# Storing the outputs of layer 1's chunks 0 to 6 tile by tile instead of a chunk at a time

## The chip, the cores and the metric

The kernel runs on one core of one Trainium2 chip. The metric is the device time of one execution in microseconds (us); the median of several runs is compared. The profile shows one more execution, taken by the hardware profiler, with the core's engines: PE (TensorE matmul), PEld (TensorE weight load), DVE (VectorE), ACT (ScalarE), POOL (GpSimd) and SP (SyncE, which here only issues DMAs and waits).

## The reference

Two transformer-like layers with adaptive layer norms run on `x` of shape 4 x 1024 x 256 (batch, sequence, features), all in f32. Each layer adds a gated attention-like part and a gated mixture of experts to `x`. Cut to what matters:

```python
# layer 0: an attention without softmax, then a mixture of 8 experts (256 -> 1024 -> 256), top 2
x = x + ga * _L0_attn_ref(h, L0_attn_queries, L0_attn_combiners)
...
x = x + gb * _L0_ffn_ref(h, L0_ffn_W1, L0_ffn_b1, L0_ffn_W2, L0_ffn_b2, L0_ffn_Wr, L0_ffn_br)
...
# layer 1: fast weights over 8 chunks of 128 positions; a chunk's loss shrinks the weights for the next
h = _layernorm(x, axis=-1) * (1 + ca) + sa
x = x + ga * _L1_attn_ref(h, L1_attn_w0, L1_attn_w1, L1_attn_w2)
# then a mixture of 8 experts (256 -> 256), top 2, each output plus its probability, times its weight
h = _layernorm(x, axis=-1) * (1 + cb) + sb
x = x + gb * _L1_ffn_ref(h, L1_ffn_router_w, L1_ffn_expert_weights)
return x
```

The last line is what concerns us: the sum `x + gb * ...` of layer 1's experts is the kernel's output, 4 MB.

## The kernel before

**Tiling.** The sequence is cut into 8 chunks of 128 positions, one position per partition. `x` stays in SBUF in the tile `x_sb`, `[P, NC, B, D]` with P = 128 partitions, NC = 8 chunks, B = 4 batch entries and D = 256 features. A chunk is thus four tiles of 128 x 256 f32, 128 KB each, and 512 KB together. In the output's layout, `out[b, c*P : (c+1)*P, :]`, a tile is one contiguous piece of 128 rows of 1 KB.

**Stages.** Layer 0's attention comes first; then its experts run over blocks of 128 gathered rows, up to about 626 us into the span. Layer 1 goes through the chunks in order: `combine` finishes layer 0's output for the chunk, `normal` makes the layer norm, `fast` the fast weights, and `routed` picks each position's two experts. The rows of chunks 0 to 3 form a first group of (position, expert) pairs, `ga`, those of chunks 4 to 6 a second, `gb`. When a group is complete (after chunks 3 and 6), `closed` sorts its pairs by expert and `block` handles them 128 rows at a time: POOL gathers the rows, PE multiplies them by the expert's weights, ACT copies the result, and SP stores it to memory (L2289). After all blocks of a group, `combine` with the key `"c2"` brings the results home, tile by tile: two gathers by POOL (L332), a scaling by ACT (L1504), and on DVE a weighted sum (L1510), the gate (L1513) and the addition to `x_sb` (L1515). `combine` returns a list `done` with one entry per tile, the planner's piece for these DVE steps. Chunk 7 is done without gathers by `dense`: all 8 experts on all its rows, weighted on DVE (L2340, L2349), gated (L2369) and added to `x_sb` (L2370), and each of its four tiles is stored behind its own addition (L2373).

**The order of work.** Layer 1's instructions are handed to a planner, the class `Plan`. A piece has an engine, an assumed duration, the pieces it comes after, the buffer slots it holds, a rank and a lag. `Plan.run` steps through a simulated time: at each step every free engine starts the ready piece of lowest rank whose slots are free. The pieces are then issued in the order of their planned starts, and each engine, SP's queue included, executes in that order. SP takes 0.1 us for a store in this plan. Waits between engines follow from the data: SP's DMA waits for a semaphore that the writing engine raises.

**The output stores.** In the last loop, the stores of chunks 0 to 3 get ranks from 6.4 on and those of chunks 4 to 6 from 8.2 on. Each of these seven stores comes after the whole list `done` and carries the chunk's four tiles in one DMA:

```python
plan(SP, 0.1, store, after=done, rank=(6.4, 8.2)[which] + 0.2 * (q - first))
```

The store of chunk 6 is SP's last DMA. Behind it stand the closing waits, drains and barriers of the program (L2525 in the profile).

Of the kernel before, what the change touches and what calls it, by code (L numbers as in the profile page):

```python
# [19 lines left out]
P = 128  # L20
B, S, D = 4, 1024, 256
# [117 lines left out]
def adaln_d2_kernel(  # L139
# [20 lines left out]
    nc = tc.nc  # L160
# [22 lines left out]
    x_sb = const.tile([P, NC, B, D], F32, name="x_sb")  # L183
# [58 lines left out]
    rank = const.tile([P, E], F32, name="rank")  # L242
# [7 lines left out]
    for dst, sign, op in ((upto16, 1, ALU.is_ge), (past16, -1, ALU.is_gt)):  # L250
        nc.gpsimd.affine_select(
            out=dst,
# [8 lines left out]
    def iota(name, pattern, shape, base=0, mult=0, mask=None, pool=const):  # L261
# [21 lines left out]
        out=below16,  # L283
# [595 lines left out]
    plan = Plan(p1=3, p2=2, pm=3, xn1=5, h1T=2, xn2=6, h2T=2, t1=1)  # L879
# [422 lines left out]
    q = plan("SP", 0.1, gates_out, after=rows_done, rank=-0.8, lag=2.2)  # L1302
# [14 lines left out]
    for half in range(2):  # L1317
# [8 lines left out]
        rank_ = max(SECONDS) - 0.3  # L1326
# [33 lines left out]
    d = of_batch["turned"]  # L1360
# [3 lines left out]
    def bases():  # L1364
# [3 lines left out]
    d = plan(DVE, 3.9, lambda: g0.close_staged(pa), after=[m], holds=[ps], rank=-1.0)  # L1368
# [4 lines left out]
        after=[m2],  # L1373
        holds=[ps2],
        rank=-0.9,
# [4 lines left out]
    d = plan(DVE, 1.4, lambda: g0.limits(pa), after=[m, bs], holds=[ps], rank=-1.0)  # L1380
    plan(DVE, 1.2, lambda: g0.list_weights(pa), after=[d], holds=[ps], rank=-0.75)
    for j in range(AHEAD):
# [11 lines left out]
        first = -1.0 + 0.1 * j  # L1394
# [47 lines left out]
    SP = "SP"  # L1442
# [320 lines left out]
    plan = Plan(rings=RINGS, **room1)  # L1763
# [184 lines left out]
    plan = Plan(rings=RINGS, **room1)  # L1948
# [199 lines left out]
    def shares(g, c, at, vb, x, rank):  # L2148

        key = ("m", c)  # L2150

        def do():
            x = made[key, "x"]
            down = tiny([P, B, E + 1], "rdown")
            nc.vector.tensor_scalar(down, x, -1.0, 1.0, ALU.mult, ALU.add)
            nc.vector.reciprocal(down, down)
            nc.vector.scalar_tensor_tensor(x, x, 1.0, down, ALU.add, ALU.mult)
            p = tiny([P, 2, B], "rp")
            nc.vector.tensor_reduce(p[:, 0, :], x[:, :, :E], AX.X, ALU.add)
            nc.vector.reciprocal(p[:, 0, :], p[:, 0, :])  # L2160
            nc.vector.tensor_tensor(
                p[:, 1, :].unsqueeze(2), x[:, :, E : E + 1], p[:, 0, :].unsqueeze(2), ALU.mult
            )
            total = tiny([P, B], "rtotal")
            nc.vector.scalar_tensor_tensor(
                total, p[:, 0, :], 1e-6, p[:, 1, :], ALU.add, ALU.add
            )
            nc.vector.reciprocal(total, total)
            w = g.w[:, :, at : at + B]
            nc.vector.tensor_tensor(  # L2170
                w, p, total.unsqueeze(1).to_broadcast([P, 2, B]), ALU.mult
            )
            nc.vector.tensor_tensor(p, p, w, ALU.mult)
            nc.vector.tensor_tensor(vb[:, at : at + B], p[:, 0, :], p[:, 1, :], ALU.add)

        return plan(DVE, 2.2, do, after=[x[0]], holds=[x[1]], rank=rank)
# [5 lines left out]
    def closed(g, after, rank):  # L2182

        key = g.name
        ps = plan.slot("pm")

        def turn():
            made[key, "turn"] = g.turn(ps_m, 0)

        def bases():  # L2190
            made[key, "bases"] = g.bases(ps_m)

        def ranks():
            made[key, "ranks"] = g.ranks(ps_m)

        m = plan(PE, 0.3, turn, after=after, holds=[ps], rank=rank)
        t = plan(
            ACT, 0.7, lambda: g.turned(made[key, "turn"], 0), after=[m], holds=[ps], rank=rank
        )
        ps = plan.slot("pm")  # L2200
        m = plan(PE, 0.15, lambda: g.total(ps_m), after=[t], holds=[ps], rank=rank)
        d = plan(DVE, 2.3, lambda: g.close(late), after=[m], holds=[ps], rank=rank)
        ps = plan.slot("pm")
        m = plan(PE, 0.15, bases, after=[t], holds=[ps], rank=rank)
        b = plan(
            ACT, 0.2, lambda: g.based(made[key, "bases"]), after=[m], holds=[ps], rank=rank
        )
        ps = plan.slot("pm")
        m = plan(PE, 0.4, lambda: g.across(ps_m), after=[d], holds=[ps], rank=rank)
        e = plan(DVE, 0.2, g.list_experts, after=[m], holds=[ps], rank=rank)  # L2210
        d = plan(DVE, 1.1, lambda: g.limits(late), after=[e, b], holds=[ps], rank=rank)
        ps = plan.slot("pm")
        m = plan(PE, 0.3, ranks, after=[t], holds=[ps], rank=rank + 0.3)
        s = plan(
            DVE,
            0.8,
            lambda: g.places(late, made[key, "ranks"]),
            after=[m],
            holds=[ps],
            rank=rank + 0.3,  # L2220
        )
        s = plan(DVE, 0.8, lambda: g.slots(late), after=[d, s], rank=rank + 0.5)
        return d, e, s

    def block(g, j, rows, y, lists, experts, stored, rank):
# [65 lines left out]
        m = plan(PE, 0.87, mm, after=[a], holds=[xTs, p2], rank=rank)  # L2291
        a = plan(ACT, 0.45, out_, after=[m], holds=[p2, ys], rank=rank - 0.2)
        s = plan(SP, 0.35, store, after=[a], holds=[ys], rank=rank - 0.2)
        return moved(0.5, [s], rank - 0.4, [ys], 1.6)

# [91 lines left out]
    for c in range(NC):  # L2387
        if c in firsts:
            slot, slotT, ts = plan.slot("h1"), plan.slot("hT1"), []
            plan("BEFORE", 0.0, lambda: None, holds=[slot, slotT], rank=-9.0)  # L2390
        else:
            sums = combine(
                "c1",
                c,
                "yg1",
                None,
                g0,
                lambda b, c=c: c * B + b,
                None,
                gb0,  # L2400
                [],
                c - 1.3,
                2.7,
            )
            slot, slotT, hs, ts = normal(
                ("n1", c), c, "1", [[d] for d in sums], (SHA, SCA), c - 1.2, [range(B)]
            )
        sums, decay = fast(c, slot, slotT, ts, lasts["decay"])
        lasts["decay"] = decay
        slot, slotT, hs, ts = normal(  # L2410
            ("n2", c), c, "2", [[d] for d in sums], (SHB, SCB), 7.65 if c == NC - 1 else c + 0.92, [range(B)]
        )
        which = 0 if c < 4 else 1
        if c == NC - 1:
            d, x = routed(last_pairs, c, 0, slotT, ts, 7.46)
            dense(c, slotT, ts, d, x, 8.23)
            continue
        g, first = groups[which], 4 * which
        at = (c - first) * B
        d, x = routed(g, c, at, slotT, ts, c + 1.05)  # L2420
        shares(g, c, at, vbs[which], x, c + 1.5)
        lasts[which].append(d)

        def store(c=c, at=at, which=which):
            nc.sync.dma_start(
                rows_of[which][at * P : (at + B) * P, :].rearrange("(b p) d -> p b d", p=P),
                made["n2", c, "h"],
            )

        stored[which].append(  # L2430
            plan(SP, 0.1, store, after=hs, holds=[slot], rank=c + 1.1, lag=3.5)
        )
        if c in (3, 6):
            lists, experts, slots = closed(g, lasts[which], c + 0.97)
            base, span = ([4.57, 1.5], [7.35, 0.66])[which]
            ys = [
                block(
                    g,
                    j,
                    rows_of[which],  # L2440
                    y_of[which],
                    lists,
                    experts,
                    stored[which],
                    base + span * j / g.J,
                )
                for j in range(g.J)
            ]
            for q in range(first, c + 1):
                done = combine(  # L2450
                    "c2",
                    q,
                    "yg2",
                    y_of[which],
                    g,
                    lambda b, q=q, first=first: (q - first) * B + b,
                    vbs[which],
                    mods1[GB],
                    [*ys, slots],
                    (6.49, 7.89)[which] + 0.2 * (q - first),  # L2460
                )

                def store(q=q):
                    nc.sync.dma_start(
                        out[:, q * P : (q + 1) * P, :].rearrange("b p d -> p b d"),
                        x_sb[:, q, :, :],
                    )

                plan(SP, 0.1, store, after=done, rank=(6.4, 8.2)[which] + 0.2 * (q - first))
    with tc.manual_schedule(engines=ORDERED | {EngineType.SP}):  # L2470
        plan.run()

# [56 lines left out]
```

## Time and profile before

| | |
|---|---|
| median of 5 runs | 1130.69 us (1130.35 to 1132.93) |
| the profiled execution, its own time | 1131.56 us |
| span of the profiled execution | 1129.8 us |
| granted TensorE clock, mean | 0.992 |
| PE busy | 1090.7 us (97%) |
| DVE busy | 589.0 us (52%) |
| ACT busy | 424.3 us (38%) |
| POOL busy | 422.2 us (37%) |
| software DMA queue (POOL's gathers and scatters) | 31872 packets, 69.68 MB |
| hardware DMA queue (SP's DMAs above all) | 44622 packets, 49.92 MB |
| stores of L2464, start of the first four | 980.9 to 1018.3 us |
| stores of L2464, start of the last three | 1105.1, 1117.3 and 1125.2 us |
| stores of L2373 (chunk 7) | 1095.0, 1111.5, 1121.6 and 1123.9 us |

Busy times of different engines overlap, so they don't add up to the span. A group in the profile names the line, the engine, the operation, what is written and read, a count and a mean duration. A DMA has three times: SP's issue, the packets on the DMA engines, and the landing, when the last of its semaphore counts has arrived. Times in the views are counted from the start of the span.

### The profile page before, as it was taken

How to read it: one execution, taken by the hardware profiler on the slowest of the kernel's cores; microseconds unless marked ns; L12 is line 12 of the kernel's file. 1: busy time of each engine (PE TensorE's matmuls, PEld its weight loads, DVE VectorE, ACT ScalarE, POOL GpSimd, SP SyncE). 2: the span in 40 equal slices, each digit the busy share in tenths (PEclk: the TensorE clock that was granted, in tenths of full speed). 3: DMA queues.
4: the chain of work that ended last, by engine and by line, in shares of the span. 5: the costliest groups of instructions: out<-in, count | busy, mean ns of one | idle time of the engine just before them, and what ended most of it. 6: DMA issues, size and time to landing. Idle time of an engine off the chain costs nothing.

```text
span 1129.8 us, 18450 instructions
## 1 busy us (share of the span) xinstructions
PE 1090.7 (97%) x6231; PEld 869.4 (77%) x6231; DVE 589.0 (52%) x2305; ACT 424.3 (38%) x1148; POOL 422.2 (37%) x483
## 2 busy tenths in 40 slices
PE   8999999999999999999999999999999999999994
PEld 5997799999999999999989565675656667656761
DVE  7777332222222222222257488968577635798567
ACT  5976233322333222333234333423224425342431
POOL 1000455555555555555454010100114422754635
PEclk8999999999999999999999999999999999999998
DMA  9425439433241514242161211100013323432544
GB/s 318 160 54 98 146 131 323 152 113 117 87 147 36 191 37 152 78 128 102 38 227 64 72 57 57 59 25 19 1 33 95 119 69 85 131 116 80 162 108 147
DMA packets 77692, 122.38 MB, mean 108 GB/s; under 512 B 27340, under 2 KB 57301, under 8 KB 72990
## 3 DMA queue, kind: packets, MB, share of 16 engines
q0 software_dynamic: 31872, 69.68, 20.0%
q1 hardware_dynamic: 44622, 49.92, 14.2%
q10 hardware_dynamic: 1104, 1.58, 0.4%
q8 instruction: 52, 0.85, 0.3%
q14 instruction: 42, 0.34, 0.1%
HBM read 205.25 MB, written 30.22 MB: 208 GB/s over the span
## 4 chain that ended last, share of the span: by engine, by line
PE 84%; DVE 8%; DMA 4%; ACT 2%; issue 2%; POOL 0%; SPq 0%; ACTq 0%; DVEq 0%
PE p_h L1658 20%; PE p_y L1681 19%; PE p_u L1967 19%; PE p_f L2015 10%; PE p_e L2276 5%; PE pm_x L2259 1%; DMA w<-in_W,g_wrow 1%; PE pm_x L1638 1%; PE pm_l L2107 1%; PE pm_t L1620 1%; PE pm_gram L1100 1%; PE pm_counts L737 1%; DMA yg<-y 1%; PE pm_l L1233 1%; PE pm_o L1193 1%
## 5 line engine op out<-in xcount | busy, mean ns | idle before, releaser
L1670 ACT ACTIVATE hid<-p_h,w 128x128 f32<-128x128 f32 x544 | 154.9, 368 | 324.2 <-issue 262.4
L1658 PEld LDWEIGHTS p_h<-xT,w 128*128 128x128 f32 x2176 | 253.1, 192 | 6.0 <-DVE xT L1643 2.1
L1658 PE MATMUL p_h<-xT,w 128*128 128x128 f32 x2176 | 254.4, 275 | 2.1 <-DVE xT L1643 1.5
L1681 PE MATMUL p_y<-w,hid 128*128 128x256 f32 x1088 | 248.9, 382 | 0.0
L1967 PE MATMUL p_u<-hT,a 128*128 128x512 f32 x512 | 230.8, 595 | 1.7 <-ACT hf L1979 0.9
L1681 PEld LDWEIGHTS p_y<-w,hid 128*128 128x128 f32 x1088 | 201.7, 190 | 24.5
L1967 PEld LDWEIGHTS p_u<-hT,a 128*128 128x128 f32 x512 | 94.4, 190 | 98.2 <-issue 88.3
L332 POOL DMA_INDIRECT w<-in_W,g_wrow x134 | 134.9, 1007 | 74.4 <-ACT hid L1670 46.3
L784 POOL DMA_INDIRECT y<-y,g_dest x68 | 69.5, 1022 | 146.8 <-DVE g_reached L724 112.2
L1643 DVE COPY xT<-pm_x 128x256 f32<-128x256 f32 x68 | 28.8, 423 | 179.7 <-PE pm_x L1638 179.7
L1692 DVE TENSOR_TENSOR y<-p_y,w 128x256 f32<-128x256 f32 x68 | 28.8, 424 | 175.2 <-PE p_y L1681 175.2
L2015 PE MATMUL p_f<-a,hf 128*128 128x256 f32 x512 | 116.1, 380 | 0.0
L332 POOL DMA_INDIRECT xg<-h_rows,g_row x68 | 66.7, 981 | 123.5 <-DVE g_hits L750 103.1
L2015 PEld LDWEIGHTS p_f<-a,hf 128*128 128x128 f32 x512 | 96.3, 190 | 17.7 <-issue 5.7
L2063 POOL TENSOR_TENSOR x_sb<-x_sb,step 128x256 f32<-128x256 f32 x32 | 24.4, 762 | 174.1 <-DVE step L2056 120.6
L332 POOL DMA_INDIRECT xg<-ga_rows,ga_row x39 | 37.3, 956 | 91.3 <-DVE ga_row L759 34.4
L2276 PE MATMUL p_e<-ew,xT 128*128 x280 | 70.5, 384 | 0.3 <-ACT y L2286 0.3
L1979 ACT ACTIVATE hf<-p_u,decay 128x512 f32<-128x512 f32 x56 | 38.1, 684 | 78.1 <-PE p_u L1967 74.2
L2276 PEld LDWEIGHTS p_e<-ew,xT 128*128 128x128 f32 x280 | 49.4, 190 | 9.5 <-issue 3.3
L1578 DVE TENSOR_TENSOR h<-h,mod 128x256 f32<-128x256 f32 x128 | 51.5, 426 | 7.8 <-ACT h L1568 5.5
L1983 DVE SCALAR_TENSOR_TENSOR hf<-p_u,decay,hf 128x512 f32<-128x512 f32 x56 | 41.9, 748 | 22.7 <-PE p_u L1967 15.4
L2286 ACT COPY y<-p_e 128x256 f32<-128x256 f32 x70 | 25.9, 371 | 59.8 <-PE p_e L2276 27.6
(362 smaller groups left out, 1285.7 us busy)
## 6 DMA issues: line engine op xcount, KB each, us to landing
yg<-y SPq DMA_DIRECT2D x32, 256.0 KB, 2.5
ga_y<-y SPq DMA_DIRECT2D x39, 128.0 KB, 1.7
x_sb<-in_x SPq DMA_DIRECT2D x8, 512.0 KB, 7.6
h_rows<-xn SPq DMA_DIRECT2D x8, 512.0 KB, 4.3
gb_y<-y SPq DMA_DIRECT2D x31, 128.0 KB, 1.7
out_x<-x_sb SPq DMA_DIRECT2D x7, 512.0 KB, 3.7
a<-in_fw SPq DMA_DIRECT2D x6, 512.0 KB, 9.6
mod<-mod_rows SPq DMA_DIRECT2D x6, 512.0 KB
```

Source lines behind the costliest of these rows:

```text
L332: return nc.gpsimd.indirect_dma_start(out=dst, out_offset=None, in_=table, in_offset=bass.IndirectOffsetOnAxis(ap=index, axis=0), bounds_c ...
L784: nc.gpsimd.indirect_dma_start(out=table, out_offset=bass.IndirectOffsetOnAxis(ap=dest, axis=0), in_=y, in_offset=None, bounds_check=2 * s ...
L1578: nc.vector.tensor_tensor(h, h, mods1[(sc, sh)[i]][:, b, :], (ALU.mult, ALU.add)[i])
L1643: nc.vector.tensor_copy(xT, pt)
L1658: nc.tensor.matmul(p1[:, i, :], lhsT=w1[:, k * H + m * P : k * H + (m + 1) * P], rhs=xT[:, k, :], start=(k == 0), stop=(k == KD - 1),)
L1670: nc.scalar.activation(hid[:, m, :], p1[:, i, :], AF.Relu, bias=w1buf[j % 2][:, KD * H + m : KD * H + m + 1],)
L1681: nc.tensor.matmul(p2, lhsT=hid[:, m, :], rhs=w2[:, m * D : (m + 1) * D], start=(m == 0), stop=(m == KH - 1),)
L1967: nc.tensor.matmul(pu, lhsT=a[:, k, m * P : (m + 1) * P], rhs=made["n1", c, "hT"][:, k, :, :], start=(k == 0), stop=(k == KD - 1),)
L1979: nc.scalar.activation(made[key, m], made[key, m, 0], AF.Silu, scale=decays[c])
L1983: nc.vector.scalar_tensor_tensor(h, made[key, m, 1], decays[c], h, ALU.mult, ALU.mult)
L2015: nc.tensor.matmul(made[key, "p2", b], lhsT=made[key, m][:, b * P : (b + 1) * P], rhs=a1[:, m, :], start=(m == 0), stop=(m == KH - 1),)
L2276: nc.tensor.matmul(made[key, "p2"], lhsT=made[key, "xT"][:, k, :], rhs=ew_flat[:, bass.ds(made[key, "at"] + k * D, D)], start=(k == 0), st ...
```

## The change

The loop over the chunks of a group gets an inner loop over the four tiles. Where one store per chunk waited for all four entries of `done`, a store per tile waits for that tile's entry alone, with the same rank and the same assumed duration. The bytes stored are the same; the number of DMAs goes from 7 to 28. Chunk 7's stores are as before.

```diff
-                def store(q=q):
-                    nc.sync.dma_start(
-                        out[:, q * P : (q + 1) * P, :].rearrange("b p d -> p b d"),
-                        x_sb[:, q, :, :],
-                    )
-
-                plan(SP, 0.1, store, after=done, rank=(6.4, 8.2)[which] + 0.2 * (q - first))
+                for b in range(B):
+
+                    def store(q=q, b=b):
+                        nc.sync.dma_start(
+                            out[b, q * P : (q + 1) * P, :], x_sb[:, q, b, :]
+                        )
+
+                    rank_ = (6.4, 8.2)[which] + 0.2 * (q - first)
+                    plan(SP, 0.1, store, after=[done[b]], rank=rank_)
```

## The prediction

> **What bounds the kernel now.** I read the views in this order: the busy time by engine, the chain of waits in its last microseconds, SP's waits, two windows around the last addition, and the transfers of the last two stores.
>
> ```profile
> span 1129.8 us, 18450 instructions
> ...
> PE 84%; DVE 8%; DMA 4%; ACT 2%; issue 2%; POOL 0%; SPq 0%; ACTq 0%; DVEq 0%
> ...
> out_x<-x_sb SPq DMA_DIRECT2D x7, 512.0 KB, 3.7
> ```
>
> Over the whole span TensorE sets the time, so what matters is whether the seven chunk stores stand on the chain anywhere, and they can only do so at the end. The chain's last steps, and two windows cut where the last addition ends:
>
> ```profile
> 1121.19 0.41 DVE x_sb L2370
> 1121.60 0.04 issue
> 1121.64 0.50 DVE yg L1510
> ...
> 1123.41 0.04 DVE x_sb L2370
> 1123.45 0.31 issue
> 1123.76 0.49 DVE yg L1510
> 1124.24 0.02 issue
> 1124.27 0.43 DVE yg L1513
> 1124.70 0.02 issue
> 1124.73 0.42 DVE x_sb L1515
> ```
>
> ```profile
> 1093.00:1125.20 32.20, 20.82 (x48) 8.67 (x47) 30.22 (x70) 7.20 (x12) 21.55 (x22) 0.91 0.47 143
> 1125.20:1129.80 4.60, 0.00 (x0) 0.00 (x0) 0.00 (x0) 0.00 (x0) 0.00 (x0) 0.50 0.35 116
> ```
>
> The columns after the length are PE, PEld, DVE, ACT and POOL busy (with counts), the clock, the DMA share and GB/s. From 1093 to 1125.2 DVE is busy 30.22 of 32.20 us, so DVE sets this stretch. Then for 4.6 us no engine computes. What fills them is the last chunk store and the closing of the program:
>
> ```profile
> SPq L2525 <- DMA out_x<-x_sb: 2.6, 1, 2.6
> ```
>
> SP issues the store of chunk 6 at 1125.18 (0.38 us of issue) and its closing waits stand 2.6 us on that store, until 1128.44. After that come seven more closing waits of SP, from 1128.52 to 1128.89, and 0.94 us of drains and barriers to 1129.84.
>
> **The change part by part.**
>
> *The last store.* Before, it carries 512 KB; after, its place is taken by a store of one tile, 128 KB, which waits for the same last addition. The other three tiles of chunk 6 have been added by 1119.50, 1120.82 and 1123.04, so they leave up to 5.7 us sooner. A 128 KB store of the same shape is in the trace four times, from L2373:
>
> ```profile
> L2373 SPq DMA_DIRECT2D out_x<-x_sb x4: 332/332/338, 1095.0 to 1123.9; - x4
> ...
> DMA to landing us min/median/max: 1.9/1.9/1.9
> ```
>
> The view gives a landing for only part of them. The trace's semaphore records give all: 1.72, 1.92, 1.87 and 1.69 us from the start of the issue, against 3.16, 3.30 and 3.25 for the last three chunk stores. The rate of traffic shows where that lies. This is the 6 us from 1125, in slices of 0.15 us, where only the chunk store moves after the second slice:
>
> ```profile
> GB/s 219 7 0 0 0 0 0 177 362 328 348 369 348 348 335 328 362 178 68 0 0 0 0 0 0 0 0 0 0 0 0 0 0 0 0 0 0 0 0 0
> ```
>
> First bytes come 0.9 us after the issue began, the transfer lasts 1.8 us (12 slices), and the last semaphore follows 0.6 us later. In the same records the tile store issued at 1123.87 has its first bytes after 0.83 us and a transfer of 0.52 us. So three quarters of the bytes are worth 1.2 to 1.3 us of transfer, and the rest of the difference is the confirmation of the last packets. From 3.25 I subtract 1.69, the row nearest to the new case, because it too runs after the last gather has landed: **1.56 us less**. With the slowest of the four rows, 1.92, it is 1.33.
>
> A rule speaks for less. The Trainium skill, "DMA: Bandwidth & Descriptors", section "Anatomy of one DMA", gives a fit for DMAs issued by GpSimd: about 2.0 us and the bytes over 436 GB/s. By it 512 KB take 3.2 us and 128 KB 2.3 us, an estimate of 0.9 us less in place of 1.56. The trace's four rows for SP lie below its fixed part, and I go by them.
>
> *SP's closing waits.* SP's DMAs signal eight semaphores in turn, and the closing waits go through these eight in a fixed order. In the records the last store uses the first of the eight, so seven waits (0.45 us, 0.064 each) follow its landing. The change adds 3 DMAs for each of 7 chunks, 21 in all, and 21 is 5 more than a multiple of 8: the last store moves to the sixth place, with two waits behind it. That takes away 5 x 0.064 = **0.32 us**. Bounds: if the turn doesn't hold, nothing at the last place (0.45 less) and nothing gained at the first (0).
>
> *DVE's stretch before it.* The gathers that POOL issues share the DMA engines with the stores. By the semaphore records the gathers issued at 1106.20 and 1117.62, just after a chunk store, land after 3.3 and 3.9 us, the undisturbed ones after 2.8. The second one reaches DVE too late: in the chain above the step from L2370 to L1510 takes 0.45 us at 1121.19 and 0.35 at 1123.41. A tile store does far less: the gather issued at 1111.30, beside the tile store of 1111.46, takes 2.84 against 2.77 for its neighbours. So the 0.1 us goes: **0.10 us less**. New neighbours for the last gather (issued 1120.17, landed 1122.99) are the tile stores of 1119.53 and 1120.84; DVE needs it by 1123.66, so 0.67 us are spare, against 0.07 as just read and 1.1 at most (the cost of the large store). Cost 0, at worst 0.4.
>
> *SP's issue time.* 28 stores at 0.33 us are 9.3 us in place of 7 x 0.38 = 2.7. SP waits for DVE before every one of them, and tile additions in the tail are at least 0.8 us apart (two of different lines, 1120.82 and 1121.61), so each issue, with its wait on the semaphore used eight DMAs ago, is over before the next addition ends. Without that cover the last store would start one issue late, 0.4 us. Behind the new waits on SP stand the row store of chunk 6 (L2425, issued at 1008.48) and the expert stores from 1037 on; the additions they are queued behind come before theirs on DVE anyway, and the first expert store is 19 us after the last store of chunk 3. Cost 0.
>
> *Order on the other engines.* The planner places pieces by rank and readiness. Nothing waits for an output store, and the new pieces hold no slots; each takes 0.1 us of SP only. So the order on PE, ACT, DVE and POOL should stand. For chunks 0 to 3 the stores fall between 981 and 1019, where PE is busy 40 of 40 us (980 to 1020) and waits for no one: nothing to gain or lose.
>
> **Sum:** 1.56 + 0.32 + 0.10 = 1.98 us less. The profiled execution took 1131.56 us with a span of 1129.8, the rest lying around it; the median of the five runs, 1130.69, is 0.87 below. 1131.56 - 1.98 - 0.87 gives **1128.7 us**, 0.18% less. About 0.2%, or 2.26 us, is what a measurement of this kernel can tell from no change, so this falls just inside it.
>
> **Rivals.**
>
> *A clear gain (faster by over 0.2%).* The same mechanism with its larger bounds: landing 1.56, closing waits 0.45, and DVE's tail freed further. DVE is idle 1.98 us between 1093 and 1125.2, so there is room for 0.3 to 0.6 us beyond what I could name. Sum 2.3 to 2.6: 1128.1 to 1128.4 us. For it: three terms that all point one way, and a forecast only 0.3 us from the bound. Against it: DVE's other idle time is spread in steps of 0.02 to 0.04 us between dependent instructions, which no store touches.
>
> *Small gain or none.* The store's landing is mostly fixed, or the closing order brings nothing: 1.33 + 0 - 0.4 for a late gather gives 0.9, or 1129.8 us. Against it: all four rows of 128 KB lie under 2 us. If the change didn't take effect at the end, because SP held the three earlier tiles back, the time would stay at 1130.7; SP's queue has idle time of over 1 us before almost every store, which speaks against that.
>
> *Slower: the gathers of the tail.* Twelve tile stores now fall among 24 gathers from 1094 to 1125 where three chunk stores stood. If each cost a gather what a chunk store costs (0.5 to 1.1 us), the ACT and DVE steps fed by it would be late once the delay passes the slack, which in the records is 1.2 us at its smallest (the product of ACT's L1504 that ends at 1122.56 and is used at 1123.76). It decides when two such delays meet on one gather in most tiles: 12 x 0.5 = 6 us late, less 1.98, or +4.0: 1134.7 us. Against it: the 0.07 us read beside a tile store, and the DMA share of 0.47 in that stretch. And what bounds the last 4.6 us is one landing, not a rate. The page named above has a table, "Rules for kernel authors", that asks for many small transfers to be joined into one large one, which speaks against the whole change; its mark for mostly overhead is 64 KB, half a tile store, and the four rows of L2373 show 128 KB landing sooner than 512 KB.
>
> **How the numbers follow.** Forecast with its neighbour of a smaller gain, all within 0.2%: 0.62. Clear gain: 0.31. Slower by over 0.2%: 0.07. The predicted time is that of the likeliest, 1128.7 us. The range goes from 1128.0 (the clear gain's 1128.1 and the runs' own scatter) to 1129.9 (the small gain's 1129.8); the runs before lie within 0.3 us of their median but for one.
>
> **What would show it.** Right: the same instructions in the same order on PE, ACT, DVE and POOL; 28 stores from the changed line, each with some 1.7 to 1.9 us to landing; SP's closing wait on the last one about 1.0 us instead of 2.6; two closing waits behind it instead of seven; L2370 to L1510 at 0.35 us everywhere; a stretch without computing of about 2.7 us instead of 4.6. Wrong: another order of instructions on DVE or PE, a gather in the tail landing after 3.3 us or more with DVE waiting for it, or a last tile store that lands later than 2 us.

## The result and the profile after

| | before | after |
|---|---|---|
| median | 1131.43 us (1129.02 to 1134.03, 51 runs) | 1130.23 us (1128.09 to 1133.76, 28 runs) |
| the profiled execution, its own time | 1131.56 us | 1130.43 us |
| span | 1129.8 us | 1128.7 us |
| granted TensorE clock, mean | 0.992 | 0.991 |

The ratio after to before is 0.9991, with a 95% interval from 0.9985 to 0.9997: 1.0 us less, between 0.3 and 1.7. The forecast was 1128.7 us, 1.98 less than before's median of five runs.

From the page of the changed kernel, the span, the shares of the chain and the output stores:

```profile
span 1128.7 us, 18492 instructions
...
PE 83%; DVE 8%; DMA 4%; issue 2%; ACT 2%; POOL 0%; SPq 0%; ACTq 0%; DVEq 0%
...
out_x<-x_sb SPq DMA_DIRECT2D x32, 128.0 KB, 1.8
```

The instructions grow by 42 (18450 to 18492): 21 stores, and one wait of SP for each. PE, DVE, ACT and POOL have the same instructions in the same order. The 32 stores are 28 of the changed line and 4 of chunk 7.

The two windows around the end of the last addition, changed kernel, columns as before:

```profile
1093.00:1125.15 32.15, 21.11 (x48) 8.66 (x46) 30.05 (x70) 7.20 (x12) 21.75 (x22) 0.84 0.53 155
1125.15:1128.70 3.55, 0.00 (x0) 0.00 (x0) 0.00 (x0) 0.00 (x0) 0.00 (x0) 0.50 0.11 37
```

The stretch without computing shrank from 4.60 to 3.55 us, not to the 2.7 of the forecast. DVE still fills the stretch ahead of it. SP's wait on the last store, from the view of waits of the changed kernel:

```profile
SPq L2527 <- DMA out_x<-x_sb: 0.8, 1, 0.8
```

It fell from 2.6 to 0.8 us, more than the whole gain. So the shorter store is there, and something takes over behind it. The line of the program's closing shows what. There each engine's queue has instructions that the trace calls DRAIN, and barriers behind them. Here are the DRAINs of POOL and SP in the kernel before; the columns are shortest/median/longest duration in ns, then the start of the first and the last:

```profile
L2525 POOLq DRAIN  x3: 40/113/14772, 1112.9 to 1129.6; - x3
L2525 SPq DRAIN  x3: 7/7/7, 1129.0 to 1129.3; - x3
```

And in the changed kernel:

```profile
L2527 POOLq DRAIN  x3: 40/113/14435, 1113.4 to 1128.4; - x3
L2527 SPq DRAIN  x3: 7/7/7, 1127.1 to 1128.1; - x3
```

SP reaches its first closing DRAIN 1.9 us sooner: 1127.1 in place of 1129.0. POOL's long DRAIN does not move with it. Its record begins while the last gathers are still being issued and ends at 1112.9 + 14.77 = 1127.7 before and 1113.4 + 14.44 = 1127.8 after (1127.63 and 1127.88 in the trace's records). Before, that was 1.4 us ahead of SP and hidden (SP's second closing DRAIN starts at 1129.02, behind all its waits). After, it is 0.8 us behind SP (1127.11), and the last barrier waits for it. From the later of the two the end follows after 0.82 us in both kernels.

The chain of waits, changed kernel, at the last tile:

```profile
1120.42 3.20 DMA yg<-gb_y,gb_slot
1123.62 0.03 issue
1123.65 0.02 DVEq L1510
1123.67 0.04 issue
1123.72 0.50 DVE yg L1510
```

The last gather lands at 1123.62, against 1122.99 before, and now DVE waits for it: its L2370 ends at 1123.52 and L1510 starts 0.2 us later. The chain here runs through POOL's gathers and no longer through DVE alone. These gathers, 24 of them for the tiles of chunks 4 to 6, are called the tail gathers below.

### The profile page after: what moved, and what is told of

Its sections match the earlier page's. It is cut to its first block, busy times and chain, and to the rows that moved or that the text cites. A ratio compares the mean times of both kernels' runs of the same rounds, so it can differ in the third digit from the quotient of the medians.

```text
span 1128.7 us, 18492 instructions
## 1 busy us (share of the span) xinstructions
PE 1090.5 (97%) x6231; PEld 869.1 (77%) x6231; DVE 588.4 (52%) x2305; ACT 424.6 (38%) x1148; POOL 422.3 (37%) x483
## 4 chain that ended last, share of the span: by engine, by line
PE 83%; DVE 8%; DMA 4%; issue 2%; ACT 2%; POOL 0%; SPq 0%; ACTq 0%; DVEq 0%
PE p_h L1658 20%; PE p_y L1681 20%; PE p_u L1967 19%; PE p_f L2015 10%; PE p_e L2276 4%; PE pm_x L2259 1%; DMA w<-in_W,g_wrow 1%; PE pm_x L1638 1%; PE pm_l L2107 1%; PE pm_t L1620 1%; DVE ln_st L948 1%; PE pm_counts L737 1%; PE pm_l L1233 1%; PE pm_o L1193 1%; DMA x_sb<-in_x 1%
```

## The experiments

The theory (A) is this: the end comes 0.82 us after the later of two events, SP's passing of its closing waits (the start of its second closing DRAIN) and the end of POOL's long closing DRAIN, and that DRAIN ends a set time after the end of the last gather's issue. The rivals have the missing 0.8 us as fixed work behind the stores, or as chance in one profile. A second question was why the last gather came later.

The experiments fell on five chips. On one of them the kernel before took 1131.22 us, close to the 1131.43 above. On the other four it took 1148.36 to 1152.69 us. There DVE stands 9.9 to 14.2 us in the tail before its use of products of chunk 7, so that POOL is done long before SP, whatever the kernel. The last part of this document shows these waits. On those four chips the whole gain of SP's part can be seen, but POOL's DRAIN cannot set the end.

**First set: one gather less, one more, and chunk 6 alone.** `after_drop` uses the first expert's rows twice for chunk 6's last tile:

```diff
-                if y is not None:
+                if y is not None and (key, c, b, i) == ("c2", 6, B - 1, 1):
+                    got.append(got[0])
+                elif y is not None:
...
+                other = 0 if (key, c, b) == ("c2", 6, B - 1) else 1
```

`after_extra` and `before_extra` put one more gather behind the last tail gather:

```diff
+    def more():
+        gather(tiny([P, D], "extra", 1), y_of[1], groups[1].slot[:, 1, 11:12])
+
+    plan(POOL, 1.28, more, after=done[-1:], rank=50.0)
```

`only6` splits the store of chunk 6 and leaves the other six as they were:

```diff
+                if q in (6,):
+                    for b in range(B):
...
+                        plan(SP, 0.1, store, after=[done[b]], rank=rank_)
+                else:
```

> The changed kernel without the last of POOL's 24 tail gathers: the second expert's rows for the last tile of chunk 6 aren't fetched, the first expert's stand in for them; the same DVE and ACT instructions. Theory A (POOL's closing drain, 6.44 us after the end of its last gather, holds the end of the changed kernel; SP is through 0.77 us sooner): the drain ends 1.25 us sooner, SP becomes the last again, and the stretch from the start of the first tail gather to the end of the span goes from 37.92 us to about 37.1 (0.8 less, a little more if DVE's wait of 0.27 us for that gather goes too). Theory B (the changed kernel's shortfall against the forecast comes from gathers and DVE slowed by the tile stores, and the drain is only an idle record): 0.3 us less at most, 37.6 us.

> The changed kernel with one more gather on POOL behind the last one, into a tile that nobody reads. Theory A: 1.25 us (0.95 of issue and 0.30 between two) on the chain that sets the end: the stretch from the first tail gather to the end goes from 37.92 to about 39.2 us, and POOL's drain still ends 6.44 us after the last gather's issue. Theory B: no change within 0.2 us, since nothing waits for the gather's data.

> The kernel before with the same additional gather. Theory A: POOL's drain was over 1.4 us ahead of SP's closing waits in the kernel before; one gather moves it by 1.25 us, so the end stays: stretch 39.1 us, at most 0.1 more. If the end moved by the full 1.25 us here too (40.4 us), the barrier would wait for POOL for another reason than its place in time, and theory A would fall.

> Only chunk 6 is stored tile by tile, chunks 0 to 5 as before. Theory A with the semaphore turn: 3 DMAs more, so the last store is in the fourth of the eight places and four closing waits follow it; SP is through 0.12 us later than in the changed kernel, still before POOL. POOL's gathers start as in the kernel before (no shift in the turn before them) and meet fewer tile stores, so the drain ends some 0.2 to 0.4 us sooner against the first landing of the tail than in the changed kernel: stretch 37.5 to 37.9 us. Theory C (all 28 small stores are needed for what was gained): stretch about 38.5 or more.

This chip was one of the four: the stretch from the first tail gather to the end took 45 to 49 us, not the 37 to 39 of the expectations. Ratios, in this order: 0.9989 (0.9970 to 1.0009), 0.9992 (0.9977 to 1.0006), 0.9994 (0.9975 to 1.0013) and 0.9982 (0.9968 to 0.9997). POOL's DRAIN ended 3.6 to 6.3 us ahead of SP in all four, so the rivals were not told apart. Two things could be read. The DRAIN ends 6.36 us after the end of the last gather's issue with 23 tail gathers, 6.53 with 25, and 6.44 with 24. And with SP last the change brings what the forecast had for SP: from the last addition to the end 4.72 us in `before_extra` and 2.80 in `after_extra`, 1.92 less.

**Second set, on the chip like the first: many gathers, the other half of the change, earlier gathers.** `after_extra6` and `before_extra6` issue six more gathers behind the last one, so that POOL is last in both:

```diff
+    for i in range(6):
+
+        def more():
+            gather(buf("xg", [P, D]), y_of[1], groups[1].slot[:, 1, 11:12])
+
+        plan(POOL, 1.28, more, after=done[-1:], rank=50.0)
```

`upto5` splits chunks 0 to 5 and leaves the last store whole (`if q in (0, 1, 2, 3, 4, 5):` in place of `only6`'s condition). `after_early` gives the blocks of the second group earlier ranks, so that the tail's gathers start earlier:

```diff
-            base, span = ([4.57, 1.5], [7.35, 0.66])[which]
+            base, span = ([4.57, 1.5], [7.35, 0.6])[which]
```

> The changed kernel with six more gathers on POOL behind the last one, into row buffers that nobody reads any more: 7.5 us more on POOL (6 x 1.25). In the first set of runs, on a chip where DVE's tail was some 8 us longer, SP was the last in all four kernels, so nothing told the theories apart; six gathers are enough to put POOL last on either chip. Theory A (the closing barrier waits for POOL's drain, 6.4 us after the end of its last gather's issue): the end of the span comes 7.3 us (6.44 + 0.04 + 0.78, rounded) after the last gather's issue ends, whatever SP does, and SP's drain stands idle until then. Theory B (POOL's drain doesn't hold the end): the end comes 2.8 us after the last addition, as in the runs after_drop and after_extra.

> The kernel before with the same six gathers. Theory A: its end too comes 7.3 us after the last gather's issue ends, and no longer 4.7 us after the last addition; with POOL last in both, this kernel and the changed one with six gathers have the same tail within 0.5 us, although their last stores differ. Theory B: 4.7 us after the last addition.

> Chunks 0 to 5 are stored tile by tile, chunk 6 as a chunk: all of the change but its last store. If the gain sits in the last store and its place among the eight semaphores: 18 more DMAs put the last store in the third place, with five closing waits behind it, and the end comes 4.6 us after the last addition (4.69 less 2 x 0.06), against 2.8 to 2.9 with chunk 6 split. If the earlier stores carry the gain, it would be 3.6 us or less.

> The changed kernel with the blocks of the second group ranked closer together (0.60 for 0.66), so that the planner finishes the last block sooner and POOL's tail gathers start about 1.2 us sooner by the plan; PE's, DVE's and ACT's orders change a little around it. Theory A: where POOL is the last in the changed kernel (the chip of the first profiles), the end comes up to 0.8 us sooner and SP is last again, 2.8 us after the last addition; where DVE's tail is the longer one, nothing is gained but what the order gives. Theory B: no gain on either chip.

The closing lines of the four, `after_extra6` first:

```profile
L2533 POOLq DRAIN  x3: 40/113/8753, 1130.1 to 1139.4; - x3
L2533 SPq DRAIN  x3: 7/7/7, 1134.3 to 1139.1; - x3
```

`before_extra6`:

```profile
L2531 POOLq DRAIN  x3: 40/113/9347, 1126.7 to 1136.6; - x3
L2531 SPq DRAIN  x3: 7/7/7, 1131.9 to 1136.3; - x3
```

`upto5`:

```profile
L2536 POOLq DRAIN  x3: 40/113/14482, 1116.2 to 1131.6; - x3
L2536 SPq DRAIN  x3: 7/7/7, 1131.0 to 1131.3; - x3
```

`after_early`:

```profile
L2527 POOLq DRAIN  x3: 40/112/13863, 1117.0 to 1132.7; - x3
L2527 SPq DRAIN  x3: 7/7/7, 1132.1 to 1132.4; - x3
```

The end of POOL's long DRAIN is its start and its longest duration, as above. The same from the trace's records, in us:

| kernel | POOL's DRAIN ends | SP is past its closing waits | the kernel ends | behind the later one | last addition to end |
|---|---|---|---|---|---|
| before | 1127.63 | 1129.02 | 1129.84 | 0.82 | 4.69 |
| after | 1127.88 | 1127.11 | 1128.71 | 0.83 | 3.58 |
| `after_extra6` | 1138.83 | 1134.35 | 1139.65 | 0.82 | 11.53 |
| `before_extra6` | 1136.05 | 1131.97 | 1136.86 | 0.82 | 11.45 |
| `upto5` | 1130.67 | 1131.07 | 1131.89 | 0.82 | 4.22 |
| `after_early` | 1130.87 | 1132.16 | 1132.98 | 0.82 | 2.80 |

The pair with six gathers more, profiled once each (1141.36 us changed, 1138.85 before), decides it. With POOL last in both, the end comes 7.75 us after the end of the last gather's issue with tile stores and with chunk stores, and the stretch from the first tail gather to the end is 45.92 and 45.83 us. The 1.9 us of SP's part are gone. The 7.3 us that were expected took the DRAIN's 6.44 us from 24 gathers; with 30 it was 6.93. `after_early` is the reverse: its SP is last again, by 1.3 us, and its end comes 2.80 us behind the last addition, not 3.58. So the 0.8 us are not fixed work behind the stores. But it was not the earlier gathers that made SP the last there. The profiled execution, 1134.71 us, is the slowest of ten (median 1130.85), and from the first tail gather to the last addition DVE took 36.2 us in it, against 34.3 in the changed kernel's profile; from the first tail gather to the end of POOL's DRAIN it was 36.89 us, against 37.10. So 1.9 us of the turn came from a later DVE and 0.2 from POOL. The time did not fall either: 0.9998 (0.9988 to 1.0007). That earlier gathers are worth anything is not shown.

`upto5` (1133.61 us, one execution) places the gain in chunk 6's store. With that one whole, SP still waits 2.2 us on it, from its view of waits:

```profile
SPq L2536 <- DMA out_x<-x_sb: 2.2, 1, 2.2
```

Its 0.47 us (4.22 for 4.69, where 4.6 had been expected) are a landing of 2.93 us in place of 3.25, and two closing waits fewer behind it. The waits were expected. The landing was not: chunk 6's whole store took 2.93 to 3.50 us to land in the four profiles that have it, and why is not shown.

**Third set: the changed kernel again, chunk 6 alone again, chunks 4 to 6.** `after_drop2`, `after_again` and `only6_again` repeat kernels; `last3` has `if q in (4, 5, 6):`.

> Again the changed kernel without the last of POOL's 24 tail gathers (the second expert's rows for the last tile of chunk 6 aren't fetched, the first expert's stand in for them). The profiles so far agree with one rule: the end comes 0.78 us after the later of SP's drain and POOL's drain. Where the tail is the short one of the first profiles (some 34 us from the first tail gather to the last addition), POOL's drain ends 1.33 us sooner without this gather (1.25 for the gather, 0.08 for a shorter drain), SP is last, and the end comes 2.8 us after the last addition in place of 3.58: stretch from the first tail gather to the end about 37.0 us, 0.8 to 1.0 less than the changed kernel's 37.92. Where the tail is the long one, 2.8 us too, as already seen. If POOL's drain weren't the reason for the 3.58, it would stay at 3.3 us or more on the short tail.

> The changed kernel itself, to stand beside the others on one chip. Short tail: POOL's drain last, the end 3.3 to 3.6 us after the last addition, time about 1.0 us under the kernel before. Long tail: SP last, the end 2.8 us after the last addition, about 1.9 us under.

> Only chunk 6 stored tile by tile. The small stores of chunks 0 to 3 shift the turn of the eight semaphores by 12, so that in the changed kernel three more of POOL's waits follow the last expert store before the first tail gather (0.94 us from its landing to the gather, 0.73 in the kernel before); here the shift isn't there: 0.73 us. On the short tail POOL's drain is last too, and the end comes 0.1 to 0.4 us sooner against the last expert store's landing than in the changed kernel (38.86 us from that landing to the end there, 39.84 in the kernel before). Time: 1.0 to 1.5 us under the kernel before.

> Chunks 4 to 6 stored tile by tile, 0 to 3 as chunks: 9 more DMAs, so the last store is in the second of the eight places, six closing waits follow its landing, and SP's drain comes 0.25 us later than in the changed kernel (2.24 us after the last addition, 1.99 there); 0.73 us from the last expert store's landing to the first tail gather, as in the kernel before. If the turn of the semaphores isn't what sets these numbers, they stay at 1.99 and 0.94.

Again one of the four chips (1152.11 us before): SP was last everywhere, and the gathers' question stayed unanswered. `after_drop2` took 1151.32 and `last3` 1152.30 us (one execution each), `after_again` 0.9997 (0.9978 to 1.0016), `only6_again` 0.9992 (0.9976 to 1.0009). From the last addition to the end it was 2.80, 3.05, 2.81 and 2.92 us. These steps are SP's closing waits: the last store's semaphore is in the sixth of eight places in the whole change, in the fourth with chunk 6 alone and in the second with chunks 4 to 6, as their numbers of DMAs say (21, 3 and 9 more; 5, 3 and 1 above a multiple of eight). With chunks 4 to 6, SP is past its closing waits 2.24 us after the last addition, as expected, and 1.99 us in the changed kernel.

This set, with all the others, settled why the first tail gather starts later. It waits for the last `gb_y` store. From that store's landing to the gather's start it is 0.728 us (0.727 to 0.728) in the eight profiles of kernels that leave chunks 0 to 3 whole, and 0.938 us (0.937 to 0.939) in the twelve of kernels that split them. The 12 DMAs more of chunks 0 to 3 move that store to another semaphore. In the kernel before, the wait that this landing ends is POOL's last ahead of the gather; in the changed kernel two more come behind it, 0.087 us apart. So splitting chunks 0 to 3 costs 0.21 us at the start of the tail's gathers.

**Fourth and fifth set: once more for the deciding run.** The kernels are the three of before: `after_drop`'s, `only6`'s and the changed one.

> The changed kernel without its last gather (the second expert's rows of chunk 6's last tile), once more, for a chip on which the stretch from the first tail gather to the end is about 38 us and not 45. Theory A (POOL's closing DRAIN ends 6.36 us after the last gather issue here, 6.44 with 24 gathers, and ends the kernel when it is later than SP): POOL's drain comes some 1.3 us sooner (one gather of 0.95 us, a gap of 0.30 and 0.08 of drain), so SP is last, last addition to end is 2.80 us and not 3.58, and the stretch from the first gather to the end is 36.9 to 37.2 us and not 37.92. Rival B (the 3.58 us are fixed work behind the stores): 3.58 us again, stretch 37.65 to 37.9. On a chip with the long tail both give 2.80 us and nothing is told apart.

> Chunk 6 alone tile by tile, chunks 0 to 5 whole, for a chip with the short tail. Theory A: the last gb_y store stays on the semaphore that it has in the kernel before, so the first gather starts 0.728 us behind its landing and not 0.938, and POOL's closing DRAIN, which is last, comes 0.21 us sooner relative to that landing than with the whole change: landing to end 38.4 to 38.7 us against 38.86; ratio 0.9987 to 0.9992 (the whole change 0.9991). Last addition to end about 3.2 to 3.6 us. Rival (the splitting of chunks 0 to 5 is worth something by itself): landing to end above 38.86, ratio above 0.9995. With the long tail SP is last: 2.92 us from last addition to end.

> The whole change once more beside the other two. Theory A, short tail: POOL's DRAIN last, 7.27 us from the end of the last gather's issue to the end, last gb_y store's landing to first gather 0.938 us, ratio about 0.9991. Rival (the missing 0.8 us were chance in one profile): last addition to end 2.80 us here, SP last. With the long tail SP is last by either.

> The changed kernel without its last gather (the second expert's rows of chunk 6's last tile). Told apart only where PE runs through the tail, so that the stretch from the first tail gather to the last addition is about 34 us: theory A 2.80 us from the last addition to the end, rival B 3.58 us. Where PE stops in the tail both say 2.80.

> Chunk 6 alone tile by tile. Last gb_y store's landing to first gather 0.728 us in any case. Theory A with PE running through the tail: landing to end 38.4 to 38.7 us against 38.86 for the whole change, ratio 0.9987 to 0.9992. Where PE stops in the tail: 2.92 us from last addition to end against the whole change's 2.80, and a ratio between 0.998 and 0.9995 as in three earlier sets; the rival, that the ratios of those sets were chance, has it at the whole change's ratio, 0.0005 either way.

> The whole change on the same chip. Theory A with PE running through the tail: POOL's DRAIN last, 7.27 us from the end of the last gather's issue to the end, last addition to end more than 2.80 us; where PE stops: 2.80 us. Ratio 0.999 to 1.000.

Both sets fell on chips with the long tail (1148.36 and 1151.65 us before). `after_drop3` and `after_drop4` (1149.74 and 1151.62 us, one execution each) both ended 2.80 us behind the last addition, as both theories say there, and so did `after_3` and `after_4` with 2.81. The changed kernel without its last gather was therefore never seen where POOL would be last, and that form of the test is open. `after_extra6` and `before_extra6` carry the verdict. The rule holds in all 20 profiles: the end comes 0.82 or 0.83 us behind the later of the two. The ratios of chunk 6 alone were 0.9978 (0.9964 to 0.9993) and 0.9984 (0.9968 to 1.0000), beside 1.0001 (0.9983 to 1.0019) and 0.9978 (0.9962 to 0.9994) for the whole change. `only6_4` was thus not below `after_4`. That splitting chunk 6 alone beats the whole change is possible by its 0.728 us, and is not shown by the times; it did not run where POOL is last.

## Why the prediction was right and wrong

*The last store: right.* Forecast 1.56 us less; measured 3.245 - 1.700 = 1.545.

*SP's closing waits: right.* Forecast 0.32; from the landing until SP was past its closing waits it took 0.598 us before and 0.260 after, 0.338 less. Two waits stand behind the store, as the count of DMAs said.

*"After that come seven more closing waits of SP, ... and 0.94 us of drains and barriers": the step that failed.* It took what follows SP's waits as fixed and did not ask what is late next once SP is 1.9 us sooner. POOL's closing DRAIN ended 1.39 us ahead of SP's last wait in the profile of before. A gain of 1.98 with nothing else moved would have been cut by 0.59 there (1.98 - 1.39), and the line of the closing showed the DRAIN, with its start and its length. It cost 0.78. Seen from POOL: of its 1.39 us to spare, 0.41 went because the last gather itself was issued that much later, counted from the landing of the last `gb_y` store, and the 0.98 left are, but for 0.01, the gain of the sum below.

*DVE's stretch: wrong in sign.* 0.10 less was forecast; counted from the landing of the last `gb_y` store, the last addition came 0.13 us later. The 0.45 us that the prediction read did become 0.35, in the step from L2370 (1120.98) to L1510 (1121.33). But the last gather's cost, taken as "Cost 0, at worst 0.4", was not 0: it was issued 0.41 us later counted from that landing (0.25 from the span's start) and took 3.20 us to land in place of 2.82, and the last step from L2370 to L1510 became 0.62 us. The later issue is the 0.21 us of the shifted semaphores, and gather issues that were 0.20 us longer in sum (23.64 for 23.44). The 0.07 us that the prediction read beside one tile store was also too low a price: five of the 24 tail gathers took 3.20 to 3.39 us to land, each with a tile store issued less than 0.9 us from its own issue, among them the last; other gathers as near to one took 2.8 to 3.1. The turn of eight was worked out for the last store alone; it also moves every DMA between, among them the one that the gathers wait for.

*The sum, counted from that landing:* 1.545 + 0.338 - 0.13 - 0.78 = 0.97 us less, where 0.78 is what the end came later behind the last addition than in kernels with SP last (3.58 for 2.80). The profiled spans differ by 1.13, because the landing itself came 0.16 sooner in the second profile (1089.84, 1090.00). The medians differ by 1.20 and the ratio gives 1.0.

*The number.* The result lies 1.53 us above the forecast. About half is the gain (1.20 instead of 1.98). The other 0.74 is the median of before, 1130.69 with the five runs shown and 1131.43 with 51. The range took the scatter from five runs "within 0.3 us of their median but for one"; 51 runs spread from 1129.02 to 1134.03.

*The signs to look for.* Right: the same order on PE, ACT, DVE and POOL, the closing wait near 1.0 us (0.8), two waits behind it, the last tile store under 2 us. Wrong: "28 stores from the changed line, each with some 1.7 to 1.9 us to landing". In the group's view for the changed kernel:

```profile
L2466 SPq DMA_DIRECT2D out_x<-x_sb x28: 332/332/338, 972.9 to 1125.2; - x28
...
DMA to landing us min/median/max: 1.7/2.2/2.7
```

The view has a landing for part of them only. By the semaphore records of all 28, 19 took 1.70 to 1.93 us and nine 2.10 to 2.71; only the last one's matters for the end, with 1.70. Wrong too: L2370 to L1510 "at 0.35 us everywhere" (0.62 at the last tile) and the 2.7 us without computing (3.55). The sign of being wrong, a gather that lands after 3.3 us or more with DVE waiting for it, was nearly met by the last gather: 3.20 us, and DVE waited 0.2. Of the rivals, the small gain came nearest: its 0.9 us have the right size, by other terms (a fixed landing, a closing order that brings nothing). The slower one failed on its price. The longest tail gather took 3.39 us to land after the change and 4.00 before, beside a chunk store.

## What to carry to other kernels

When an edit brings one engine's last event forward, list the last event of every engine and queue before crediting the gain: it is worth no more than the distance to the next one, 1.39 us here. A closing DRAIN behind gathers belongs on that list. When an edit changes the number of DMAs on a queue, work out the new place in the turn of semaphores for each DMA that somebody waits for, not only for the last.

## What was unexpected in the hardware

*POOL's closing DRAIN.* It ended 6.36, 6.44, 6.53 and 6.93 us after the end of the last gather's issue with 23, 24, 25 and 30 tail gathers, 0.08 us for each, with a spread under 0.002 us over chips. The last gather's data had landed long before (1123.62, 4.3 us ahead of the DRAIN's end, in the changed kernel). What POOL does in that time the profile does not say.

The Trainium skill, "VectorE: DVE Perf Modes", section "The DRAIN you can't avoid", gives the DRAINs that the runtime puts around a program about 12 ns on all five engines. The closing DRAINs here stand at a line of the program itself: SP's three last 7 ns each, but POOL's longest is recorded with 14.77 us before and 14.44 after. So the page's figure is no guide to them.

*The tail on four of the chips.* DVE's waits between 1100 and 1146 in `after_4`:

```profile
DVE step L2349 <- remote: 11.0, 2, 6.1
DVE step L2349 <- PE p_e L2324: 3.2, 4, 1.3
```

The stretch from the first tail gather to the last addition there, with the columns of the windows above:

```profile
1102.80:1148.30 45.50, 28.54 (x53) 10.93 (x51) 31.24 (x72) 7.20 (x12) 23.31 (x24) 0.80 0.37 112
```

And in the changed kernel's first profile:

```profile
1090.80:1125.10 34.30, 23.30 (x53) 9.61 (x51) 31.14 (x72) 7.20 (x12) 23.62 (x24) 0.85 0.51 149
```

DVE does the same work in both (31.24 and 31.14 us, 72 instructions). PE's 53 matmuls are busy 5.2 us longer (28.54 for 23.30) at a lower granted clock (0.80 for 0.85), and DVE stands 14.2 us before L2349, which uses chunk 7's products (L2324); 11.0 of it is put down to "remote", a releaser that the view does not name. So the changed kernel's end is set by POOL's DRAIN in the profile of the first chip and by SP in those of these four, and an edit at the end can be worth 1.0 us on the first and, from the last addition to the end, 1.9 us in the traces of the others (4.72 and 2.80 in the first set). The times there, with ratios of 0.9978 to 1.0001 for the whole change, do not tell the two apart. Why these chips are so was not tried.
